# A spectral layer behind attention: two spectrum slots instead of three, four kw per mixing matmul, transposes behind each bank, stores on one queue

## The chip, the cores and the metric

The kernel runs on one core of a Trainium2 chip. The metric is the device time of one execution in microseconds. A core has five engines with queues of their own: TensorE (PE; its weight loads are listed as PEld), VectorE (DVE), ScalarE (ACT), GpSimd (POOL) and SyncE (SP). SP, ACT and POOL also issue DMAs: an issue stands in order in its engine's queue, and the profile shows it under SPq, ACTq or POOLq. A line number such as L198 is a line of the kernel before.

## The reference

The input x has shape (4, 64, 96, 96). Two layers follow each other, both on a group-normalised input and both added to it.

```python
# layer 0, N = 9216 places, 8 channels for q and k
energy = einsum('bcn,bcm->bnm', Q, K)
att = sigmoid(energy)
out = einsum('bcm,bnm->bcn', V, att) + x
out = out * sigmoid(mlp(mean(out)) + mlp(max(out)))
# layer 1
u_hat = rfft2(u, norm='ortho')
top = einsum('bchw,cohw->bohw', u_hat[:, :, :16, :16], R_pos)
bot = einsum('bchw,cohw->bohw', u_hat[:, :, H-16:, :16], R_neg)
# v_hat is zero but for top and bot
y = irfft2(v_hat, s=(H, W), norm='ortho')
```

R_pos and R_neg are complex, 64 by 64 channels for each of 16 x 16 frequencies. Layer 1 thus uses 32 frequencies kh along the height and 16 frequencies kw along the width. All numbers are float32.

## The kernel before, in words

The four images are worked on in two pairs; the 128 partitions hold 2 images x 64 channels. Layer 0's attention runs over 2 pairs x 18 blocks of 512 query places x 24 bursts of 6 key tiles, 864 bursts in all. In a burst PE computes six energy tiles for the next burst (L420), ACT takes their sigmoid (L424), and PE multiplies the sigmoids of this burst by the values (L431). Other work is hung on bursts by lists (`mid`, `end`) that `place(offset, every, steps)` fills by hand. Pair 0's layer 1 (`Hidden`) is hung on the bursts of pair 1. Pair 1's layer 1 has no attention left to hide in and follows it, from L583 on: "the tail". Within the tail, Tile's scheduler may reorder instructions that don't depend on each other. Each engine's queue is then fixed and worked off in order.

Layer 1 has these stages, in both forms.

- **Forward along w and h.** PE multiplies by constants of cosines and sines. In the tail, DVE transposes blocks of 32 x 32 in between (L629, L643), with three buffers xt (L628); PE accumulates the two images' spectra in `pu` (L648).
- **Spectrum.** The spectrum is scaled by the normalisation (`rs`, from `spread`) and written into `ut` in the form in which the mixing needs it as a stationary operand: 128 partitions are (real or imaginary part) x (64 input channels), columns are kh x kw x 3 slots x 2 images. The slots hold the three variants of real and imaginary parts from which the mixing makes minus the imaginary part, the real part and the imaginary part of the result. In the tail this takes transposes of `pu` into its own order and with the two halves of the partitions swapped (L680 to L682), two scalings on ACT (L684, L685) and one on DVE (L686) for each image; `sign` (L671) holds the factors. In `Hidden` it is `along_h` with L299 and L301. `constant_mode` (L181) corrects the constant mode.
- **Mixing** (`mix`, L183 to L224). For each group q of four kh and each half of the kw, PE multiplies 32 columns of `ut` by the weights of two kw side by side (L198): 128 columns of moving operand, 4 kh in the four groups of 32 output partitions, 4 pairs of kw, so 16 matmuls for each PSUM bank. A float32 matmul is two records in the profile. Twelve of the 32 rows of a group are of use (2 kw x 6); products of one kw's spectrum with the other's weights are made and not read. The bank is copied to `vm` (in the tail by DVE and ACT in turn, L111 and L113; in `Hidden` by DVE alone), and after the second half the rows of each kh are stored to a DRAM tile `vd` (L209), 48 KB each: four stores, in the tail on SP and ACT in turn. After four q, the rows are read back as `vt` (L223), with kh on the partitions and the right blocks picked: eight loads of 64 KB, on SP and ACT in the tail, on SP in `Hidden`. The tail has three buffers `vm`.
- **Back along h.** PE multiplies `vt` by the constants `gh` (L709, in `Hidden` L314). `vt` stands twice (e = 0 and 1, for the real and the imaginary part of the result), in two arrangements of real and imaginary rows; `gh` is one block of 96 columns. In the tail the result fills eight PSUM banks, and DVE then transposes four banks of one image at a time into `z` (L713). In `Hidden` it goes through DRAM (`zd`), and `gh` has the rows h in an order such that each of four reads takes a run of rows.
- **Back along w.** PE multiplies by `gw` (L723, in `Hidden` L335), DVE adds the result to x1 (L727, L337), and the output is stored. In the tail, three PSUM tiles of 384 columns are made for each of 8 groups g, DVE adds each by itself, and after every second g three stores of 384 KB go out on SP and ACT in turn.

The weights of the mixing, 512 KB for each kh, are loaded by POOL in the tail: seven kh into places of their own and nine into x0's place ahead of time, nine into the place of `vT` while the tail runs, and seven into places of the tail's working tiles as these come free (L596, L656).

Of the kernel before, what the change touches and what calls it, by code (L numbers as in the profile page):

```python
# [40 lines left out]
P = 128  # L41
# [13 lines left out]
U = KH * KW * 6  # L55
UPAD = 26
# [8 lines left out]
SECOND = {"w1": 2 * R, "w2": P, "ident": P, "fw": 2 * KW, "fh": 4 * KH, "gh": H, "gw": 4 * W}  # L65
# [6 lines left out]
NSLOT = 7  # L72
NLATE = 3 * NSQ * P + H
# [3 lines left out]
def tile_kernel(ctx: ExitStack, tc: tile.TileContext, x, cst, late, spec, out):  # L77
# [67 lines left out]
    class Layer1:  # L145


        def __init__(self, p, gate, bank, move, queues):
            self.p, self.gate, self.bank, self.move, self.queues = p, gate, bank, move, queues
            self.vd = dram.tile([KH, 12, 2, KW // 2 * C], F32, tag=f"vd{p}", name=f"vd_{p}")  # L150
            self.vt = None
# [24 lines left out]
        def constant_mode(self):  # L176

            for rows, slot, op in ((slice(0, C), 1, ALU.add), (slice(C, P), 2, ALU.add),
                                   (slice(C, P), 0, ALU.subtract)):
                at = self.ut[rows, 2 * slot:2 * slot + 2]  # L180
                nc.vector.tensor_tensor(at, at, self.rs[rows, 2, :], op)  # L181

        def mix(self, q, half):  # L183
# [7 lines left out]

            pv = self.bank(f"pv_{self.p}_{q}_{half}")
            K4 = KW // 4
            for k in range(K4):
                kw = half * K4 + k
                for g in range(4):
                    at = ((4 * q + g) * KW + 2 * kw) * 6
                    nc.tensor.matmul(  # L198
                        pv[bass.ts(g, 32), :].rearrange("q (n k o) -> q n k o", n=2, o=C)[
                            :, :, k, :],  # L200
                        self.ut[:, at:at + 32],
                        self.wts[4 * q + g].rearrange("q (n k o) -> q n k o", n=2, o=C)[
                            :, :, kw, :], start=True, stop=True)
            vm = self.vms[q].rearrange("q (n m) -> q n m", n=2)
            self.move(vm[:, :, bass.ts(half, K4 * C)], pv.rearrange("q (n m) -> q n m", n=2))
            if half == 0:
                return
            for g in range(4):
                self.queues[g % 2].dma_start(  # L209
                    self.vd[4 * q + g].rearrange("s n m -> s (n m)"),  # L210
                    self.vms[q][32 * g:32 * g + 12, :])
            if q % 4 == 3:
                if self.vt is None:
                    self.vt = self.places_of_vt()
                row, M = 12 * KW * C, KW // 2 * C
                for b in range(2):
                    for part in range(2):
                        to = 64 * b + 32 * part + 4 * q - 12
                        for e in range(2):
                            of = self.vd[4 * q - 12, 2 * (1 - part + e) + b, 0, :]  # L220
                            of = bass.AP(tensor=of.tensor, offset=of.offset,
                                         ap=[[row, 16], [6 * KW * C + M, 2], [1, M]])
                            self.queues[e + 1].dma_start(  # L223
                                self.vt[e][to:to + 16, :].rearrange("h (n m) -> h n m", n=2), of)  # L224

    class Hidden(Layer1):


        def __init__(self, p, gate, bank, move, queues, work):
            super().__init__(p, gate, bank, move, queues + queues[:1])  # L230
# [6 lines left out]
        def places_of_vt(self):  # L237
            vt = self.work.tile([P, 2, KW * C], F32, tag="ah", name=f"vt_{self.p}")
            return [vt[:, 0, :], vt[:, 1, :]]
# [22 lines left out]
        def along_w(self, m):  # L262
# [10 lines left out]
            for g in range(4):  # L273
                self.queues[0].dma_start(
# [3 lines left out]
            self.queues[1].dma_start(self.ah[rows, :],  # L278
                                     self.ad[rows].rearrange("h k c -> h (k c)"))

        def along_h(self, i):
# [3 lines left out]
            u = self.ut[:, :U].rearrange("q (h k s b) -> q h k s b", k=KW, s=3, b=2)  # L285
# [532 lines left out]
```

## Time and profile before

| what | value |
|---|---|
| time, median of 3 runs | 3213.67 us (3213.33 to 3218.87) |
| profiled execution, its own time | 3214.8 us |
| its span | 3213.0 us |
| PE busy (matmuls) | 3145.4 us, 98% |
| ACT busy | 2435.0 us, 76% |
| DVE busy | 405.3 us, 13% |
| L431, attention times values | 10368 records of 601 ns |
| L420, energies | 5184 records of 460 ns |
| L198, mixing of pair 0 | 512 records of 273 ns (median) |
| mean granted clock of TensorE | 0.992 |

The span is the time from the first to the last instruction of the execution that was profiled; the 1.8 us more in its own time lie around it. Busy shares are averages over the whole span. As the attention fills nearly all of it, they say little of the tail, which has to be read by itself: from the end of the attention (about 3105 us) to 3213.0. The mean duration of a matmul record includes its way through the array, and records overlap, so a rate is read from the starts of consecutive records and not from the durations.

### The profile page before, as it was taken

To read this page: it belongs to the slowest core of one execution; us is meant where nothing else is said; L and a number is where in the kernel's file an instruction comes from. 1 tells how busy PE (TensorE), PEld (TensorE's weight loads), DVE (VectorE), ACT (ScalarE), POOL (GpSimd) and SP (SyncE) were. 2 spreads that over 40 slices of the span, in tenths; PEclk is the share of its full clock that TensorE was granted. 3 is DMA by queue.
4 is the path that set the end of the run, shared out by engine and by line. 5 is a ranking of instruction groups with operands and counts; after the bars stand their busy time and mean duration, and the time that the engine had idled before them with its cause. 6 is when DMAs were issued, how large, how long until landed. Compare 5 with 4: busy or idle time off the path is not lost.

```text
span 3213.0 us, 40155 instructions
## 1 busy us (share of the span) xinstructions
PE 3145.4 (98%) x17960; PEld 1076.8 (34%) x17960; DVE 405.3 (13%) x856; ACT 2435.0 (76%) x1767; POOL 20.3 (1%) x41
## 2 busy tenths in 40 slices
PE   7999999999999999999999999999999999999985
PEld 3333333333333333334333333333333333333334
DVE  5200000000000000003231110000000110000034
ACT  3788888888888888886777777777777777888861
POOL 0000000000000000000000000000000001000000
PEclk9999999999999999999999999999999999999997
DMA  3000000000000000000120101211010013000034
GB/s 138 1 1 1 1 1 1 1 1 1 1 1 1 1 1 1 1 1 1 40 92 16 38 1 43 75 63 39 16 24 20 30 40 133 1 1 1 16 98 144
DMA packets 38973, 86.85 MB, mean 27 GB/s; under 512 B 10672, under 2 KB 16816, under 8 KB 38704
## 3 DMA queue, kind: packets, MB, share of 16 engines
q1 hardware_dynamic: 31696, 60.83, 6.4%
q0 software_dynamic: 4752, 17.42, 1.5%
q10 hardware_dynamic: 2352, 6.04, 0.6%
q8 instruction: 140, 2.29, 0.3%
q14 instruction: 33, 0.27, 0.0%
HBM read 63.82 MB, written 20.45 MB: 26 GB/s over the span
## 4 chain that ended last, share of the span: by engine, by line
PE 97%; DVE 1%; DMA 1%; issue 0%; ACTq 0%; ACT 0%; SPq 0%; DVEq 0%; POOL 0%
PE acc L431 73%; PE e L420 18%; PE pv L390 1%; PE pv L198 1%; PE py L335 1%; PE pq L401 1%; PE pk L381 0%; DMA x<-in_x_dram 0%; PE py L723 0%; PE pt L257 0%; DVE x L156 0%; PE pz L314 0%; DVE xt L629 0%; DMA vt<-vd 0%; DMA vd<-vm 0%
## 5 line engine op out<-in xcount | busy, mean ns | idle before, releaser
L424 ACT ACTIVATE at<-e 128x1536 f32<-128x1536 f32 x1728 | 2412.4, 1448 | 682.1 <-PE e L420 682.1
L431 PE MATMUL acc<-at,vT 128*64 128x512 f32 x10368 | 2417.6, 601 | 0.0
L431 PEld LDWEIGHTS acc<-at,vT 128*64 128x64 f32 x10368 | 667.9, 136 | 1294.7 <-issue 1279.5
L420 PE MATMUL e<-q,kT 32*128 32x512 f32 x5184 | 635.7, 460 | 2.0 <-ACT at L424 1.3
L420 PEld LDWEIGHTS e<-q,kT 32*128 32x128 f32 x5184 | 257.2, 182 | 638.8 <-issue 588.6
L361 DVE TENSOR_SCALAR full_q<-pq,cs 128x256 f32<-128x256 f32 x36 | 17.4, 484 | 1556.7 <-PE pq L401 1556.6
L575 DVE SCALAR_TENSOR_TENSOR x<-acc,x 128x512 f32<-128x512 f32 x36 | 24.9, 692 | 293.7 <-PE acc L431 293.7
L390 PE MATMUL pv<-cs,x 128*128 128x128 f32 x288 | 42.9, 292 | 0.2
L337 DVE TENSOR_TENSOR x<-py,x 128x384 f32<-128x384 f32 x24 | 13.4, 558 | 226.1 <-PE py L335 226.1
L411 DVE CAST q<-q 32x256 fp32r<-32x256 f32 x144 | 41.0, 285 | 3.8
L390 PEld LDWEIGHTS pv<-cs,x 128*128 128x128 f32 x288 | 35.7, 195 | 14.1 <-DVE full_k L361 12.9
L510 DVE COPY ws<-pv 128x512 f32<-128x512 f32 x16 | 11.1, 691 | 216.4 <-PE pv L198 216.4
L369 DVE SCALAR_TENSOR_TENSOR q<-high_q,cs,full_q 64x256 fp32r<-64x256 f32 x72 | 34.6, 481 | 2.4
L510 DVE COPY xT<-pt 96x512 f32<-96x512 f32 x24 | 16.4, 685 | 114.4 <-PE pt L257 114.4
L361 DVE TENSOR_SCALAR full_k<-pk,cs 128x256 f32<-128x256 f32 x36 | 17.4, 484 | 102.0 <-PE pk L381 102.0
L392 DVE TENSOR_TENSOR vT<-pv,cs 128x512 f32<-128x512 f32 x36 | 24.9, 691 | 8.8 <-PE pv L390 8.8
L577 DVE TENSOR_REDUCE maxs<-x 128x1 f32<-128x512 f32 x36 | 24.7, 685 | 1.1
L381 PE MATMUL pk<-x,cs 128*64 128x256 f32 x144 | 23.0, 390 | 1.5 <-DVE x L143 1.5
L637 PE MATMUL pa<-xt,lc 128*128 128x256 f32 x72 | 20.0, 432 | 3.4 <-DVE xt L629 3.4
L438 DVE BATCH_NORM_STATS2 stats<-x 128x6 f32<-128x512 f32 x36 | 22.2, 679 | 7.9 <-DMA x<-in_x_dram 7.9
L401 PE MATMUL pq<-x,cs 128*64 128x256 f32 x144 | 22.1, 386 | 0.0
L335 PE MATMUL py<-cs,ws 128*128 128x384 f32 x48 | 21.9, 538 | 0.0
(99 smaller groups left out, 450.2 us busy)
## 6 DMA issues: line engine op xcount, KB each, us to landing
ws<-in_spec_dram SPq DMA_DIRECT2D x32, 512.0 KB
x<-in_x_dram SPq DMA_DIRECT2D x15, 512.0 KB
out_dram<-x SPq DMA_DIRECT2D x18, 384.0 KB
w<-in_spec_dram POOLq DMA_DIRECT2D x10, 512.0 KB, 4.9
old<-in_x_dram SPq DMA_DIRECT2D x12, 384.0 KB
x1d<-x SPq DMA_DIRECT2D x12, 384.0 KB
x<-x1d SPq DMA_DIRECT2D x12, 384.0 KB
w_early<-in_spec_dram POOLq DMA_DIRECT2D x9, 512.0 KB, 9.1
```

What stands on the lines that cost most here:

```text
L198: nc.tensor.matmul(pv[bass.ts(g, 32), :].rearrange("q (n k o) -> q n k o", n=2, o=C)[:, :, k, :], self.ut[:, at:at + 32], self.wts[4 * q + ...
L335: nc.tensor.matmul(py[:, :4 * W], self.z[:, i, :], named("gw"), start=True, stop=True)
L361: nc.vector.tensor_scalar(u, src, bias, None, ALU.add)
L369: mark[0] = nc.vector.scalar_tensor_tensor(dst, h.bitcast(F32), is_low, u, ALU.mult, ALU.add)
L390: nc.tensor.matmul(pp[:, bass.ts(i, P)], xs[p][:, bass.ts(4 * s + i, P)], named("wv"), start=True, stop=True)
L392: nc.vector.tensor_tensor(vT[:, 4 * s:4 * s + 4, :], pp.rearrange("p (i m) -> p i m", m=P), named("bv").unsqueeze(1).to_broadcast([P, 4, P ...
L401: nc.tensor.matmul(pq[rows, :half], named("wq")[:, rows], xs[p][:, n * NB + e * half:n * NB + (e + 1) * half], start=True, stop=True)
L411: nc.vector.tensor_copy(q[to:to + 32, cols], q[of:of + 32, cols])
L420: nc.tensor.matmul(eb[i // PART][:, i % PART, :], kT[r:r + 32, t // 4, :], q[r:r + 32, :], start=True, stop=True)
L424: nc.scalar.activation(at[:, bass.ts(h, PART), :], eb[h], AF.Sigmoid)
L431: nc.tensor.matmul(acc[half, :], vT[:, j, half], at[:, i, :], start=(j == 0), stop=(j == NCH - 1))
L510: l1 = Hidden(0, gate, bank_a, lambda dst, src: nc.vector.tensor_copy(dst, src), (nc.sync, nc.sync), work)
```

## The change

The spectrum `ut` has two slots (the real part's and the imaginary part's product) instead of three. The minus sign moves into `gh`, which gets two blocks, one for each e, and `vt` stands once. In the mixing, SIDE = 4 kw lie side by side: a matmul has the same 32 columns of stationary operand, of which 16 are now of use, and 256 columns of moving operand, and a bank takes 2 x 4 matmuls instead of 4 x 4. A store of `vd` has 16 rows (64 KB) instead of 12, and all of them are on SP; four loads of `vt`, in pieces of 1 KB, take the place of eight in pieces of 2 KB. In the tail the loads after q = 3 are on POOL, those after q = 7 on SP and ACT. There are four `vm` and four xt.

Back along h in the tail goes by groups of 16 output channels: for each group, two e and two images, matmuls of 256 columns that read `vt` with a step of 64 elements, each image's group into a bank of its own; behind each bank stands a transpose of 512 elements. Back along w, one addition takes the three PSUM banks of a g, and the three stores follow it. One kh less is loaded ahead of time (NSLOT 6) and one more late. In `Hidden`, the two scalings of `along_h` are split by n instead of by slot, and the reads of `zd` take every fourth row, as `gh` has its rows in plain order.

```diff
-U = KH * KW * 6
-UPAD = 26
+SIDE = 4
+U = KH * KW * 4
+UPAD = 4 * SIDE
...
-            for k in range(K4):
-                kw = half * K4 + k
+            for k in range(2):
+                kw = half * 2 + k
                 for g in range(4):
-                    at = ((4 * q + g) * KW + 2 * kw) * 6
+                    at = ((4 * q + g) * KW + SIDE * kw) * 4
...
             for g in range(4):
-                self.queues[g % 2].dma_start(
-                    self.vd[4 * q + g].rearrange("s n m -> s (n m)"),
-                    self.vms[q][32 * g:32 * g + 12, :])
+                nc.sync.dma_start(self.vd[4 * q + g], self.vms[q][32 * g:32 * g + 4 * SIDE, :])
...
                 for b in range(2):
-                    for part in range(2):
-                        to = 64 * b + 32 * part + 4 * q - 12
-                        for e in range(2):
-                            of = self.vd[4 * q - 12, 2 * (1 - part + e) + b, 0, :]
...
+                    for slot in range(2):
+                        to = 64 * b + 32 * slot + 4 * q - 12
+                        of = self.vd[4 * q - 12, 2 * slot + b, :]
...
+                        self.load_queue(q, slot).dma_start(
+                            self.vt[to:to + 16, :].rearrange("h (n m) -> h n m", n=SIDE), of)
...
-                    evacuate, (nc.sync, nc.scalar, nc.sync))
+                    evacuate, lambda q, slot: nc.gpsimd if q == 3 else (nc.sync, nc.scalar)[slot])
...
-            xt = place_of(f"t{s % 3}", f"xt_{s}")[:, :STRIP]
+            xt = place_of(f"t{s % 4}", f"xt_{s}")[:, :STRIP]
...
-            nc.vector.transpose(own, pu[b])
-            nc.vector.transpose(swapped[:C, :], pu[b][C:, :])
-            nc.vector.transpose(swapped[C:, :], pu[b][:C, :])
...
+            nc.vector.transpose(tb, pu[b])
+            tb = tb.rearrange("q (n k h) -> q n k h", n=SIDE, h=KH)
+            nc.scalar.activation(u[:, :, :, :, 0, b], tb, AF.Copy, scale=l1.rs[:, 0, b:b + 1])
+            nc.vector.tensor_scalar(u[lo, :, :, :, 1, b], tb[hi], l1.rs[hi, 1, b:b + 1], None,
+                                    ALU.mult)
+            nc.vector.tensor_scalar(u[hi, :, :, :, 1, b], tb[lo], l1.rs[lo, 0, b:b + 1], None,
                                     ALU.mult)
...
-        l1.vms = [tail.tile([P, KW * C], F32, tag="vm", bufs=3, name=f"vm_{q}")
+        l1.vms = [tail.tile([P, KW * C], F32, tag="vm", bufs=4, name=f"vm_{q}")
...
+        for i in range(4):
+            for e in range(2):
+                for b in range(2):
+                    rows = bass.ts(b, 2 * KH)
+                    nc.tensor.matmul(
+                        pz[b][i][:H, :].rearrange("q (o e k) -> q e o k", e=2, k=KW)[:, e],
+                        named("gh")[rows, bass.ts(e, H)],
+                        l1.vt[rows, :].rearrange("q (k o) -> q o k", o=C)[:, bass.ts(i, NO), :],
+                        start=True, stop=True)
+        z = tail.tile([P, SQ, P], F32, tag="z", name="z_1")
         for i in range(4):
             for b in range(2):
-                rows = bass.ts(b, 2 * KH)
-                nc.tensor.matmul(pz[b][:H, bass.ts(i, NB)], gh[rows],
-                                 l1.vt[i // 2][rows, bass.ts(i % 2, NB)], start=True, stop=True)
-        z = tail.tile([P, SQ, P], F32, tag="z", name="z_1")
-        for b in range(2):
-            nc.vector.transpose(z[:H, :, bass.ts(b, C)].rearrange("q h o -> q o h"),
-                                pz[b][:H, :].rearrange("q (k o) -> q o k", o=C))
+                nc.vector.transpose(
+                    z[:H, :, b * C + i * NO:b * C + (i + 1) * NO].rearrange("q h o -> q o h"),
+                    pz[b][i][:H, :])
...
-            for j in range(NSQ):
-                part = x1[:, bass.ts(j * (SQ // HG) + g, HG * W)]
-                nc.vector.tensor_tensor(part, py[j][:, :HG * W], part, ALU.add)
-                if g % 2:
+            nc.vector.tensor_tensor(rows_of[:, g], py[:, :, :HG * W], rows_of[:, g], ALU.add)
+            if g % 2:
+                for j in range(NSQ):
```

## The prediction

> **What bounds the kernel now.** I read the shares by engine and the slices of the page first, then the chain that ended last, then the busy time by stretch, and last the timeline of the stretches that the change touches.
>
> ```profile
> PE 3145.4 (98%) x17960; PEld 1076.8 (34%) x17960; DVE 405.3 (13%) x856; ACT 2435.0 (76%) x1767; POOL 20.3 (1%) x41
> ...
> PE 97%; DVE 1%; DMA 1%; issue 0%; ACTq 0%; ACT 0%; SPq 0%; DVEq 0%; POOL 0%
> ```
>
> TensorE (PE) carries 97% of the chain, nearly all of it attention (L431, L420). Pair 0's spectral layer is hidden there by DVE and the queues, but its matmuls lie on PE's own path. Pair 1's spectral layer stands bare behind the attention, from 3105 to 3213 us. So there are two questions: what the change does to PE inside the attention, and what it does to the bare 108 us. For the first, the timeline of PE around one hidden mixing step:
>
> ```profile
> 1950.29 0.73 PE L420 MATMUL e<-q,kT 32*128 32x512 f32 x6
> 1950.95 2.79 PE L431 MATMUL acc<-at,vT 128*64 128x512 f32 x12
> 1953.68 1.08 PE L198 MATMUL pv<-ws 128*32 128x128 f32 x32
> 1954.69 0.73 PE L420 MATMUL e<-q,kT 32*128 32x512 f32 x6
> ```
>
> A burst with a half step of mixing lasts 1954.69-1950.29 = 4.40 us; without one, 3.39 (1950.29-1946.90). So each of the 16 half steps costs 1.01 us of end time. For the second, the bare stretch cut where its releasers stand (columns: stretch, length, busy time of PE, PEld, DVE, ACT, POOL, then clock, DMA share, GB/s):
>
> ```profile
> 3142.30:3149.84 7.54, 0.32 (x8) 0.26 (x9) 6.90 (x19) 4.45 (x4) 1.10 (x2) 0.82 0.33 109
> 3149.84:3179.19 29.35, 16.54 (x512) 16.03 (x513) 5.53 (x8) 4.68 (x8) 0.53 (x1) 0.79 0.59 118
> 3179.19:3192.82 13.63, 7.35 (x16) 3.64 (x16) 7.03 (x2) 0.00 (x0) 0.00 (x0) 0.75 0.01 2
> 3192.82:3213.00 20.18, 14.15 (x192) 13.91 (x192) 11.89 (x24) 0.00 (x0) 0.00 (x0) 0.50 0.61 235
> ```
>
> These are spectrum, mixing with its round trip through DRAM, back along h, back along w. In the first DVE is the bound, 6.90 of 7.54. In the second PE works 16.5 of 29.4 and is idle for the last 12. In the third PE and DVE work strictly one after the other: 7.35+7.03 is more than 13.63. In the fourth PE is busy at half clock. Why the second is so long, the timeline of ACT shows:
>
> ```profile
> 3162.55 0.58 ACT L113 COPY vm<-pv 128x512 f32<-128x512 f32 x1 [0.65 <-PE pv L198]
> 3162.61 0.30 ACTq L209 DMA_DIRECT2D vd<-vm  x1
> 3163.20 2.75 ACTq L223 DMA_DIRECT2D vt<-vd  x4
> 3167.48 1.90 ACTq L209 DMA_DIRECT2D vd<-vm  x3
> 3169.42 0.58 ACT L113 COPY vm<-pv 128x512 f32<-128x512 f32 x1 [6.29 <-DMA vt<-vd]
> 3170.20 0.58 ACT L113 COPY vm<-pv 128x512 f32<-128x512 f32 x1 [0.20 <-DMA vd<-vm]
> ```
>
> ACT empties a PSUM bank only after the stores and first loads queued ahead on it, and the third vm buffer is not free before its stores land. PE's last product (3166.6) thus waits until 3170.2 to be copied. The chain behind it:
>
> ```profile
> 3171.58 2.88 DMA vd<-vm
> ...
> 3175.51 3.67 DMA vt<-vd
> ...
> 3179.19 6.52 PE pz L709 x13
> ...
> 3185.74 7.04 DVE z L713 x2
> ```
>
> **The change, part by part**, against the profiled execution (span 3213.0, time 3214.8, so 1.8 around it).
>
> *Hidden part: 0.* A half step has 16 matmul records of 256 columns instead of 32 of 128, four side by side either way. The tail's mixing at full clock starts one 128-column record every 27 ns, 108 ns for four, 0.85 ns a column. The 512-column acc matmuls take 2.73 us for 12, two side by side: 0.455 us, 0.89 ns a column. Narrow ones cost no more per column, so the 1.01 us stays. Bounds: half of 16.2 us if the count decided (-8), +1 if a longer chain delays a burst. I keep 0 because equal columns are the nearest row. Evictions stay 16; the back matmuls (L314) keep shape and number; along_h's DVE pair (1.125+0.64 us) becomes two of 256 elements; vt loads halve. ACT's and PE's attention work covers these DVE and SP edits (DVE is 13% busy); uncovered, they would be under 2 us in all.
>
> *Spectrum: 7.54 to 5.05, saves 2.5.* Four 64-partition transposes (0.71 each), four sign copies (0.69 together), two L686 of 0.66, one constant addition and two ACT scalings (1.17 each) go. DVE keeps two transposes (0.72 each), the four rs operations (0.42 together), four scalings on 64 partitions at L686's 0.65, and two additions (0.35): 1.44+0.42+2.60+0.35 = 4.8, with handoffs 5.05. ACT's two scalings of 1.15 fit beside. If the scalings cost like L299 (1.125), +1.9; if ACT's chain decides, -0.6. Mixing starts at 3147.35. POOL's last two weight loads are issued some 2 us earlier, 14 us before their use.
>
> *Mixing and round trip: 29.35 to 24.05, saves 5.3.* Columns are unchanged, so PE needs its 16.5 us less the stalls late in it and part of its 4 us at half clock: 15.5, to 3162.85. ACT has no store ahead of its copies and vm has four buffers, so the last copy ends 0.75 later. SP has all 32 stores. In the hidden part it issues four from 1966.80 to 1967.95, 0.38 apart, 1.5 us per q against PE's 1.75 (full clock), so it keeps up. Behind SP's stores stand only its two last vt loads, for which PE waits; the first half's four loads move to POOL, behind the weights, where nobody waits. Last store issued at 3164.75; landing 2.9 as before; semaphores and issue 0.45; two loads per queue instead of four. Before, 4.5 us passed from the first such issue (3174.68) to PE's start; the bytes are half, the pieces as many but 1 KB long. Taken 3.3: PE starts at 3171.4. Bounds: PE wholly at full clock 13.9 (-1.6), loads 2.7 to 4.5 (-0.6, +1.2), stores 0.55 apart as L209's longest on SP (+3.3, since 8x4x0.55 = 17.6 then outlasts PE). Stores carry 16 rows instead of 12, in rows of 4 KB as before.
>
> *Back along h: 13.63 to 8.8, saves 4.8.* PE streams as many columns: 16x512 records, two side by side, 4096 x 1.67 ns = 6.8 at half clock; the clock rose 5.4 us in, so about 6.4. In four groups of 1.7, two banks each. Eight DVE transposes of 512 elements: between 0.72 (L680, plain rows) and 0.94 (L643's 1877 ns for 1024, strided on both sides); the write stays strided, the PSUM read turns plain: 0.83. First group 1.9, then 8x0.83 = 6.65, handoffs 0.25: 8.8. The moving operand is now read with a step of 64 elements, which no matmul here does. Nearest is ACT's scaling with strided writes, 1.16 us for 512, 2.27 ns each against 0.58 us plain. By it PE needs 9.3 and the stage 11 (saves 2.6); by twice the half-clock rate, 13.7 and 15.3 (loses 1.7). I take 1.67, because a half-clock column already takes longer than a strided element on DVE (0.66 us/512 = 1.29 ns).
>
> Against this change speaks the Trainium skill's page "SBUF — State Buffer" (section "Door 1: The DMA port swizzle"): only accesses within one 16-byte line run at full bandwidth, each crossing pays. It gives no size; by doubling, the sum below would shrink by the 6.5 us just bounded.
>
> *Back along w: 20.18 to 19.9, saves 0.3.* One addition over 1152 elements replaces three of 384: from 550 ns for 384 and 692 for 512 follow 1.40 us against 1.49. But the six first stores wait for the whole addition (up to 0.8 us), and the last three start together at the end: +0.7 with PE at half clock. PE ran this whole stage at clock 0.50 although busy, having idled 6.3 us before. Now it idles 2.3 us and may begin at full clock. Then DVE (8x1.33) and the stores decide: 4.7 MB at the 390 GB/s reached at the end is 12.1 us, and the stage shrinks by 2.1. Nothing shows whether this sparse work holds a clock it can't raise; I take a value between.
>
> "TensorE: Matmul & The Clock Gate" (Part 1) says sustained activity of some 3.4 us raises the clock. This stage, 14 us busy at 0.50, speaks against it; by the rule the stage would run at full clock, and the sum would be 1.8 larger.
>
> The first bare stretch to 3142.3 keeps its operations; a fourth xt buffer finds DVE already the chain: 0, within 1 either way.
>
> **Sum:** 0+2.5+5.3+4.8+0.3 = 12.9: span 3200.1, profiled time 3201.9. The median of the runs shown (3213.67) lies 1.1 under the profiled time: 3200.8.
>
> **Rivals.** (1) PE stays at full clock in mixing and back along w: 1.6+1.8 more, 3197.4. For: shorter idle times; against: the last stage never left half clock. 0.18. (2) The strided moving read doubles back along h: 3207.3. For: ACT's doubled scaling; against: DVE's strided write cost only 0.66 against 0.54. 0.14. (3) One queue bounds the mixing at 0.55 us per store: 3204.1. For: L209 on SP took 0.54 to 0.56 in the mixing; against: two queues issued together then, 0.38 alone. 0.13. (4) The change doesn't do what it says: copies are still held up by another wait and the round trip gains nothing: 3206.1. 0.05. (5) Slower: that strided read at four times the half-clock price, 6.7 ns a column, adds 20.5 us: 3221.3. It decides from 1.67+12.9/4096 us, 4.8 ns a column, for no gain, and from 6.4 for a loss of 0.2%. Against: no strided row here costs over 2.3 ns. 0.05. Forecast 0.45.
>
> 0.2% is 6.4 us, about what a measurement tells from no change: below 3207.3 is faster. Half of (2) lies within 0.2%, with some of (4): faster 0.87, same 0.08, slower 0.05. The range takes in (1), (3), (4) and (2) to its middle, with the spectrum's and loads' bounds partly combined: 3195.5 to 3207.5.
>
> **What would show it.** Bursts with mixing still 4.40 us. First bare mixing matmul near 5 us after the last pu. No ACT copy waiting on a vt load. PE's idle time between mixing and pz 8.5 instead of 12.6. DVE transposes (0.8 each) beginning 2 us into pz. The prediction falls if pz records take over 1 us per 256 columns, if SP's stores lag PE by several us, or if bursts with mixing change.

## The result, and the profile after

| | before | after |
|---|---|---|
| time, median of 4 runs each | 3214.59 us (3213.33 to 3218.87) | 3205.20 us (3203.89 to 3206.90) |
| profiled execution, its own time | 3214.8 us | 3205.57 us |
| its span | 3213.0 us | 3203.8 us |

One run of the kernel before, made beside the changed one, has joined the three of the table above. The changed kernel is faster by 9.4 us: the ratio is 0.9969, with a 95% interval of 0.9951 to 0.9986. The time lies inside the range given; of the 12.9 us worked out, the profiled spans show 9.2. Lines are now those of the kernel after: L426 and L415 are the attention (before L431, L420), L198 the mixing, L209 the stores, L220 the loads of `vt`, L700 and L708 back along h, L720 and L722 back along w, L114 ACT's copies. In a kernel of an experiment these numbers shift by the lines that its edit adds.

The chain of the page, by engine, as in the line shown of before:

```profile
PE 97%; DVE 1%; DMA 1%; SPq 0%; issue 0%; ACT 0%; POOL 0%; ACTq 0%
```

SPq has moved from the seventh place to the fourth, ahead of ACT and ACTq: a first hint that the bare part now waits for SP's queue. The busy time by stretch, cut at the same events (first row: from the end of the attention to the end of `pu`; then spectrum, mixing with its round trip, back along h, back along w; columns as before):

```profile
3105.59:3142.14 36.55, 26.64 (x106) 18.36 (x108) 29.80 (x45) 12.04 (x25) 8.60 (x16) 0.89 0.62 217
3142.14:3146.89 4.75, 0.49 (x9) 0.43 (x10) 4.37 (x12) 2.08 (x2) 0.66 (x2) 0.50 0.51 183
3146.89:3173.45 26.56, 15.97 (x257) 9.35 (x257) 5.53 (x8) 4.68 (x8) 2.51 (x5) 0.82 0.56 120
3173.45:3182.65 9.20, 7.91 (x33) 5.96 (x33) 7.12 (x8) 0.00 (x0) 0.00 (x0) 0.74 0.00 0
3182.65:3203.80 21.15, 12.77 (x192) 12.35 (x192) 10.77 (x8) 0.00 (x0) 0.00 (x0) 0.56 0.58 225
```

Cut exactly at the records, that gives:

| stretch | before | after | gained | predicted |
|---|---|---|---|---|
| start to end of attention | 3105.01 | 3105.54 | -0.5 | 0 |
| to the end of `pu` | 37.28 | 36.56 | 0.7 | 0 |
| spectrum | 7.55 | 4.79 | 2.8 | 2.5 |
| mixing and round trip | 29.35 | 26.56 | 2.8 | 5.3 |
| back along h | 13.63 | 9.20 | 4.4 | 4.8 |
| back along w | 20.18 | 21.14 | -1.0 | 0.3 |
| sum | 3213.0 | 3203.8 | 9.2 | 12.9 |

Two stretches hold the difference of 3.7 us: mixing (2.5 short) and back along w (1.3 short). The hidden part did what was forecast. The timeline of PE around a hidden mixing step of the kernel after:

```profile
1951.13 0.73 PE L415 MATMUL e<-q,kT 32*128 32x512 f32 x6
1951.79 2.80 PE L426 MATMUL acc<-at,vT 128*64 128x512 f32 x12
1954.52 1.07 PE L198 MATMUL pv<-ws 128*32 128x256 f32 x16
1955.52 0.73 PE L415 MATMUL e<-q,kT 32*128 32x512 f32 x6
```

The burst lasts 1955.52-1951.13 = 4.39 us, as before (4.40), with 16 records of 256 columns in the place of 32 of 128. Here PE pays for columns, not for matmuls.

Where the mixing's gain went, the chain that ended last shows. Columns: start, length, what. The parts left out are SP's other stores, and further down the handoffs between the rows:

```profile
3153.23 0.30 SPq L209
...
3154.04 1.35 SPq L209
...
3158.22 0.42 SPq L209
...
3158.68 0.42 SPq L209
...
3161.01 1.45 SPq L209
...
3167.82 2.14 DMA vd<-vm
...
3170.21 2.99 DMA vt<-vd
...
3173.45 2.01 PE pz L700 x6
```

From 3153.23 to 3167.82 the chain is nothing but L209 on SP: fourteen and a half microseconds in which SP issues one store after another, each 0.46 from the next (3158.68-3158.22), and twice 1.35 and 1.45 us for one. PE's last mixing product was done at 3162.86 and its copy at 3163.55, both where the prediction had them (3162.85, 3163.6). The last store was issued 4.3 us after that copy. In the kernel before ACT's copies waited for their queue; now they don't. Three of them still wait for a `vm` buffer whose stores have to land first (3.5 us in all), but the last copy ends where it was expected, and the queue of the stores is the wait.

### The profile page after: what moved, and what is told of

It reads as the page before. It is cut to its first block, busy times and chain, and to the rows that moved or that the text cites. A ratio compares the mean times of both kernels' runs of the same rounds, so it can differ in the third digit from the quotient of the medians.

```text
span 3203.8 us, 39104 instructions
## 1 busy us (share of the span) xinstructions
PE 3144.6 (98%) x17464; PEld 1065.2 (33%) x17464; DVE 399.8 (12%) x838; ACT 2432.9 (76%) x1765; POOL 22.4 (1%) x45
## 4 chain that ended last, share of the span: by engine, by line
PE 97%; DVE 1%; DMA 1%; SPq 0%; issue 0%; ACT 0%; POOL 0%; ACTq 0%
PE acc L426 74%; PE e L415 18%; PE pv L385 1%; PE pv L198 1%; PE py L330 1%; PE pq L396 1%; PE pk L376 1%; DMA x<-in_x_dram 0%; PE pt L253 0%; SPq L209 0%; PE py L720 0%; PE pz L309 0%; PE pa L631 0%; PE pu L290 0%; DVE z L708 0%; PE pu L642 0%
## 5 line engine op out<-in xcount | busy, mean ns | idle before, releaser
L426 PE MATMUL acc<-at,vT 128*64 128x512 f32 x10368 | 2418.0, 601 | 0.0
L426 PEld LDWEIGHTS acc<-at,vT 128*64 128x64 f32 x10368 | 667.8, 136 | 1294.5 <-issue 1279.1
L415 PE MATMUL e<-q,kT 32*128 32x512 f32 x5184 | 636.0, 461 | 1.9 <-ACT at L419 1.3
L415 PEld LDWEIGHTS e<-q,kT 32*128 32x128 f32 x5184 | 257.5, 182 | 642.8 <-issue 591.2
L385 PEld LDWEIGHTS pv<-cs,x 128*128 128x128 f32 x288 | 35.7, 195 | 14.2 <-DVE full_k L356 12.9
```

The lines of the kernel that those rows point to most:

```text
L385: nc.tensor.matmul(pp[:, bass.ts(i, P)], xs[p][:, bass.ts(4 * s + i, P)], named("wv"), start=True, stop=True)
L415: nc.tensor.matmul(eb[i // PART][:, i % PART, :], kT[r:r + 32, t // 4, :], q[r:r + 32, :], start=True, stop=True)
L426: nc.tensor.matmul(acc[half, :], vT[:, j, half], at[:, i, :], start=(j == 0), stop=(j == NCH - 1))
```

## The experiments

All times are medians; "before" is the kernel before on the same chip. An interval of a ratio spans some 6 to 11 us between its ends, as the kernel before scatters over 5 us; so the readings below rest on the stretches, and times are compared within one chip. Where the same code ran again, the stretches repeat so: mixing 26.56, 26.66, 26.78, 27.51 (the kernel after, e13, e7, e3); spectrum 4.78 to 4.82; back along h 9.19 to 9.25; the first stretch 35.9 to 36.9; the end of the attention 3104.2 to 3106.6 us. Part of the mixing's scatter is the clock: each mixing begins at half clock, which lasts another 2.6 us (e5) to 5.5 us (e1), and PE's own part, from its first product to its last, takes 15.5 us in the one and 16.7 in the other (16.0 in the kernel after).

**The changed kernel again (e13).** It was run beside three others, to have it on their chip.

> The changed kernel itself, unedited, beside e10 to e12 on one chip. If the long issue of the last output store on ACT (1.94 us) recurs, its last stage is 21 to 21.2 us, else near 20.2; the stretch from the first mixing matmul to the first pz matmul is 26.3 to 26.9 us. By the other edits its time should lie 4 to 5 us above e10_last_q.

It took 3205.82 us (3204.20 to 3206.95); before 3215.11; ratio 0.9970 (0.9958 to 0.9981). The stretches are 26.66, 9.25 and 20.17 us. So the mixing is no accident of one execution, while one microsecond of the last stretch is: here it is 20.2 instead of 21.1. Here too two issues of SP are long (1.55 and 1.42 us).

**Stores on two queues (e1).** The change's single queue is undone for pair 1, all else stays.

```diff
-                nc.sync.dma_start(self.vd[4 * q + g], self.vms[q][32 * g:32 * g + 4 * SIDE, :])
+                (nc.sync, nc.scalar if self.p else nc.sync)[g % 2].dma_start(
+                    self.vd[4 * q + g], self.vms[q][32 * g:32 * g + 4 * SIDE, :])
```

> The changed kernel with one edit: in the tail, the mixing's stores go on SP and ACT in turn again, 16 each. Theory (SP's issue sets the end of the mixing stage: 32 stores 0.46 us apart, the last one issued 4.3 us after the last copy out of PSUM, 3167.82 against 3163.55): with two queues the last store is issued about 1.6 us after the last copy, the stretch from the first mixing matmul to the first pz matmul shrinks from 26.56 to about 24 us, and the time falls by 2 to 3 us against the changed kernel. ACT has two stores (0.95 us) and a copy (0.58) per q against PE's 1.75, so its copies stay in time. Rival (the stores' way through the DMA engines is the bound, whichever queue issues them; the engines' share is 0.45 to 0.87 there): the stretch stays at 26 to 27 us and the time doesn't move.

3202.18 us; before 3215.27; ratio 0.9959 (0.9944 to 0.9974). The mixing took 24.93, 1.6 less than with one queue. The last store was issued 0.86 after the last copy instead of 4.3. But the last copy ended 18.2 us after the stretch began instead of 16.7. Of these 1.5 us PE's longer half clock makes 0.8. The rest lies between PE's last product and the end of its copy, 1.4 us instead of 0.7: ACT issued stores until 0.1 us before that copy, and the profile puts the copy's wait down to the landing of a store. Which of the two held it was not separated. So the theory's direction held, and the full 2.5 did not come.

**One store of 128 rows per q (e2).** SP issues 8 stores instead of 32, in the hidden part too; half of the rows stored are never read. `vd` is laid out to fit.

```diff
...
-            for g in range(4):
-                nc.sync.dma_start(self.vd[4 * q + g], self.vms[q][32 * g:32 * g + 4 * SIDE, :])
+            nc.sync.dma_start(self.vd[q], self.vms[q])
...
```

> The changed kernel with one edit: for each q one store of all 128 rows of vm (512 KB, half of it rows that nobody reads) instead of four stores of 16 rows; vd is laid out to fit; in the hidden part too. SP issues 8 stores instead of 32. Theory (number of issues on SP): the last store goes out within 0.2 us of the last copy, the stretch shrinks from 26.56 to 23.5 to 24.5 us, the time by 2 to 3 us. Rival (the DMA engines): twice the bytes keep the stretch at 26.5 us or make it longer.

3202.91 us; before 3215.27; ratio 0.9960 (0.9945 to 0.9975). SP is free: the last store was issued 0.02 after the last copy. The mixing still took 24.94, because that one store landed 4.1 us after its issue, against 2.1, and PE itself took 0.6 us longer, with more of it at half clock. Twice the bytes kept the DMA engines no busier, as the DMA queues of the window from 3150 to 3170 us show (packets, MB, share of 16 engines). The kernel after:

```profile
q1 hardware_dynamic: 1024, 2.10, 56.6%
```

This kernel:

```profile
q1 hardware_dynamic: 1232, 4.27, 54.9%
```

A packet of 4 KB took 328 ns (median) in a store of 16 rows and 160 ns in one of 128.

**Three queues' worth on two (e6).** SP takes three of four stores and ACT the last one (two of the last q); the three additions of the kernel before are back too.

```diff
-                nc.sync.dma_start(self.vd[4 * q + g], self.vms[q][32 * g:32 * g + 4 * SIDE, :])
+                queue = nc.scalar if self.p and (g == 3 or (q == 7 and g == 2)) else nc.sync
+                queue.dma_start(self.vd[4 * q + g], self.vms[q][32 * g:32 * g + 4 * SIDE, :])
...
```

> The changed kernel with two edits: three additions per g back along w, and of the mixing's four stores per q one on ACT and three on SP (two and two for the last q). Theory (SP's 0.46 us per store is the bound of the mixing's end, and the joint addition that of the output's): SP needs 1.4 us per q against PE's 1.75, the last store is issued under 1 us after the last copy, the stretch from the first mixing matmul to the first pz matmul takes 23.0 to 23.7 us (26.56 with one queue, 24.93 with stores in turn), the last stage 20 to 20.2; the time is 4 to 4.5 us under the changed kernel, near 3201. Rival (the landings of these small stores are the bound, whichever queue): the stretch stays at 24.9 as with both earlier edits, time near 3202.5.

3204.53 us; before 3216.18; ratio 0.9964 (0.9951 to 0.9978). The theory fell: the mixing took 27.51, no better than with one queue, though SP had 23 stores instead of 32. What SP waited for between 3155 and 3175 us (total, times, longest):

```profile
SPq L210 <- DMA vd<-vm: 4.2, 4, 1.7
```

A store waited for the landing of an earlier store. At 3168.04 it was that of ACT's store of 3164.64, whose semaphore the waiting store uses again; SP was idle for 1.7 us, though its data were ready. The kernel after has no such row of SP. So a second limit lies close behind the issue time: stores in flight. The chain that ended last passes through four landings of stores (1.90, 2.99, 3.94 and 2.07 us), which is why cutting only the issues on SP does not help here. Some of e1's miss may lie there as well (1.7 us on two such waits). The same queues took 27.16 in e9 and 28.19 in e8, below.

**One wide store, and four small ones at the end (e10).** What e2 and e6 taught, put together: few stores (no wait for a landing), but the last q in pieces of 16 rows on two queues, which land sooner; three additions as before the change. `vd` is laid out to fit.

```diff
...
-            for g in range(4):
-                nc.sync.dma_start(self.vd[4 * q + g], self.vms[q][32 * g:32 * g + 4 * SIDE, :])
+            if q < 7 or not self.p:
+                nc.sync.dma_start(self.vd[q], self.vms[q])
+            else:
+                for g in range(4):
+                    rows = slice(32 * g, 32 * g + 4 * SIDE)
+                    (nc.sync, nc.scalar)[g % 2].dma_start(self.vd[q, rows, :], self.vms[q][rows, :])
...
```

> The changed kernel with three additions per g back along w, one store of 128 rows per q for the first seven q (as in e2_one_store), and for the last q four stores of 16 rows, two on SP and two on ACT. Theory (SP's issues up to the last q, then the landing of the last store, set the mixing's end): the last store is issued 0.5 us after the last copy, lands 2.5 us later as with two queues (4.2 with one store of 512 KB), and the stretch from the first mixing matmul to the first pz matmul takes 22.8 to 23.6 us (26.56 in the changed kernel, 24.94 with one store). With the last stage at 19 to 20 the time is 4 to 5 us under the changed kernel. Rival (the earlier 512 KB stores are still in flight and delay the last four): 24.5 us or more, as with one store.

3201.12 us (3199.95 to 3201.68); before 3215.11; ratio 0.9955 (0.9942 to 0.9967). This is the fastest kernel of the study, 14.0 us under the kernel before and 4.7 under the changed one of the same chip, whose runs begin at 3204.20. The chain at the end of its mixing:

```profile
3162.79 0.36 ACTq L213
...
3163.18 3.32 DMA vd<-vm
...
3166.60 3.00 DMA vt<-vd
```

SP no longer appears. The mixing took 24.27, between the theory's and the rival's number: the small stores queue behind the wide ones' transfers and land after 3.3 us, where 2.5 was counted on. In e11, below, the same stores landed after 2.95 us and the half clock was 1.4 us shorter: 23.20.

**The kernel before with q = 3's loads on POOL (e5).** This is the smallest edit that frees ACT's copies, made on the kernel before.

```diff
-                            self.queues[e + 1].dma_start(
+                            (nc.gpsimd if self.p and q == 3 else self.queues[e + 1]).dma_start(
```

> The kernel before with one edit: in the tail, the eight vt loads after q = 3 are on POOL instead of SP and ACT. Theory (ACT's copies stood behind the loads that wait for the stores of q = 3): the copy that waited 6.29 us for them goes at once, the stretch from the first mixing matmul to the first pz matmul shrinks from 29.35 to about 26.5 us and the time by 2.5 to 3 us. Rival (the three vm buffers, free only when the stores have landed, hold the copies as long): the stretch stays above 28.5 us.

3211.33 us; before 3215.27; ratio 0.9989 (0.9979 to 0.9998). The mixing with its round trip:

```profile
3151.30:3176.88 25.58, 15.46 (x513) 15.22 (x513) 5.54 (x8) 4.69 (x8) 4.57 (x9) 0.83 0.60 134
```

It fell from 29.35 to 25.57, more than expected. ACT's last copy moved from 3171.05 to 3167.38 and its last store from 3171.58 to 3168.06; some 0.7 us of the gain is the clock's, whose half lasted 2.6 us here against 4.1. One line thus shortens the mixing further than the whole change does (26.56).

**The same, with all stores on SP (e12).** Added to e5:

```diff
-                self.queues[g % 2].dma_start(
+                self.queues[0].dma_start(
```

> The kernel of e5_before_pool_loads (the kernel before with the loads after q = 3 on POOL) with one more edit: all stores of the mixing on SP, as in the change. Theory (one queue's issue is the cost): stores of 12 rows take 0.36 to 0.40 us on SP, four of them 1.6 against PE's 1.75 per q, so only the last q's stores come later, and the two refills of SP's instructions cost 1 us each: the stretch from the first mixing matmul to the first pz matmul rises from 25.57 to 26.2 to 27.5 us. Rival (one queue costs nothing; what was long in the changed kernel is the longer store of 16 rows): 25.4 to 25.9.

3214.67 us; before 3215.11; ratio 0.9998 (0.9989 to 1.0007): what e5 had gained is gone. The mixing takes 27.88, 2.3 more than e5's, somewhat more than expected:

```profile
3150.67:3178.55 27.88, 15.97 (x512) 15.73 (x513) 5.53 (x8) 4.68 (x8) 4.54 (x9) 0.81 0.57 124
```

Of the 2.3, PE's longer half clock makes 0.5. The chain shows L209 on SP from 3158.51 on, and then two landings:

```profile
3162.78 1.55 SPq L209
...
3166.89 4.85 DMA vd<-vm
...
3171.75 2.09 DMA vd<-vm
```

The last copy ended at 3167.96 and the last store was issued 3.8 us later. Three issues took over a microsecond each (1.03, 1.55, 1.47), and the last store then waited 0.5 us for the landing of an earlier one, as in e6. So one queue for the stores costs some 2 us also where a store has 12 rows, without the rest of the change.

**Three additions (e3).** Only the joint addition is undone; `py` is again three tiles of their own.

```diff
...
-            nc.vector.tensor_tensor(rows_of[:, g], py[:, :, :HG * W], rows_of[:, g], ALU.add)
+            for j in range(NSQ):
+                part = x1[:, bass.ts(j * (SQ // HG) + g, HG * W)]
+                nc.vector.tensor_tensor(part, py[j][:, :HG * W], part, ALU.add)
...
```

> The changed kernel with one edit: back along w uses three PSUM tiles and three additions of 384 elements for each g again, each store right behind its addition. Theory (the joint addition delays the first stores and bunches the last three; the stage took 21.15 us against 20.18 before although it began at full clock): the stage falls to about 20.2 us, the time by about 0.9. Rival (the longer stage comes from the last ACT store's issue of 1.94 us, which has nothing to do with the addition): stage within 0.4 of 21.15 if such an issue recurs there, near 19.7 if it falls elsewhere.

3203.71 us; before 3215.27; ratio 0.9963 (0.9949 to 0.9977). Back along w took 19.98. That run alone can't settle it, because the clock fell at 3181.1, just ahead of this stretch; in the kernel after it fell 2.4 us into it. Over all runs the pattern is clear. With a joint addition and a start at full clock: 20.16, 20.22, 20.17, and 21.14 and 21.06 where ACT's last output issue took 1.9 us. With three additions and a start at full clock: 18.93, 19.11, 19.40, 19.12. With three additions and half clock throughout: 19.98, 21.19, and 20.18 before (20.18 and 20.17 in e5 and e12). So the joint addition costs about a microsecond, and a start at full clock is worth about one (19.1 against 20.2; the 21.19 is taken up under e11).

**Three xt (e7).** The fourth xt buffer of the first stretch is taken back.

```diff
-            xt = place_of(f"t{s % 4}", f"xt_{s}")[:, :STRIP]
+            xt = place_of(f"t{s % 3}", f"xt_{s}")[:, :STRIP]
```

> The changed kernel with one edit: xt has three buffers again instead of four. The stretch from the end of attention to the last pu matmul took 37.28 us in the kernel before and 36.56 in the changed one, 35.9 in three variants of it. Theory A (the fourth buffer does it): the stretch goes back to 37.3 or more, the time rises by 0.7 to 1.5 us. Theory B (the phase of the clock's change does it; nothing there waits for a buffer): the stretch stays at 35.9 to 36.6.

3205.16 us; before 3216.18; ratio 0.9968 (0.9955 to 0.9980). The first stretch took 37.03, 0.1 above what four buffers gave (35.9 to 36.9). The buffer is worth nothing that this can tell.

**PE kept busy, with the strided read (e9) and with a plain one (e8).** Both have e6's queues and three additions. Nine matmuls of 512 columns, whose product nobody reads, are put behind the mixing, to raise or hold the clock for back along h. In e8 moreover PE reads `vt` in runs of 16 elements and DVE takes over the reordering. With that PE's results, too, go to PSUM in one run of 256 elements, where the kernel after and e9 write them in runs of 16 with gaps:

```diff
+        spare = l1.bank("spare")
+        for i in range(9):
+            nc.tensor.matmul(spare, ident, x1[:, bass.ts(i, NB)], start=True, stop=True)
...
-                        pz[b][i][:H, :].rearrange("q (o e k) -> q e o k", e=2, k=KW)[:, e],
+                        pz[b][i][:H, :].rearrange("q (e k o) -> q e k o", e=2, k=KW)[:, e],
...
-                        l1.vt[rows, :].rearrange("q (k o) -> q o k", o=C)[:, bass.ts(i, NO), :],
+                        l1.vt[rows, :].rearrange("q (k o) -> q k o", o=C)[:, :, bass.ts(i, NO)],
...
-                    pz[b][i][:H, :])
+                    pz[b][i][:H, :].rearrange("q (c o) -> q o c", o=NO))
```

> The kernel of e6_both with the nine dense matmuls of e8_warm_plain alone; pz reads vt with its step of 64 as in the changed kernel. Theory (the strided read holds PE at 1.69 ns a column whatever the clock): pz records stand 0.217 us apart although the clock is full, and the stage stays at 9.0 to 9.3 us. Rival (the half clock alone made them 0.217 apart; the 0.217 after the clock's rise in the changed kernel came from somewhere else): 0.11 apart, first transpose after 1.1 us, stage near 8.1.

> The kernel of e6_both with two more edits: nine dense matmuls of 512 columns, whose product nobody reads, between the last mixing matmul and the first pz matmul, so that PE doesn't idle 10 us there; and pz reads vt in runs of 16 elements instead of with a step of 64, with DVE's transposes reading PSUM with a step of 16 instead. Theory (the strided read costs 1.69 ns a column at either clock; plain reads cost 0.85 at full clock): the clock is full when pz begins, pz records stand 0.11 us apart instead of 0.217, the first transpose starts 1.1 us after pz instead of 2.03; the transposes (0.87 to 0.94 each) then are the bound and the stage falls from 9.2 to 8.1 to 8.7 us. Rival (the strided PSUM read slows the transposes to over 1 us each): 9.2 or more.

e9: 3203.58 us, ratio 0.9963 (0.9949 to 0.9976); e8: 3203.39 us, ratio 0.9964 (0.9952 to 0.9977); before 3216.18. Back along h took 9.18 and 8.98. The clock was not held: the added matmuls ended 3.7 and 3.8 us before `pz`, and it fell at 3173.1 in e9, as `pz` began, and in e8 at 3174.2, 0.7 us later. But it rose again within the stage, and so the price of the read at full clock can be seen. The busy time of the records of `pz`, cut at the clock's rise (stretch, length, busy time and records of PE, PEld, DVE, then the clock, DMA share, GB/s), first at full clock in the kernel after:

```profile
3178.23:3181.30 3.07, 3.07 (x14) 1.59 (x10) 3.07 (x5) 1.00 0.00 0
```

The same of e9, at full clock:

```profile
3176.48:3180.80 4.32, 4.32 (x20) 2.81 (x17) 4.32 (x6) 1.00 0.00 0
```

And of e8, up to the rise and from it on:

```profile
3173.52:3177.60 4.08, 4.08 (x19) 3.12 (x21) 2.44 (x3) 0.58 0.00 0
3177.60:3179.40 1.80, 1.80 (x15) 1.18 (x11) 1.80 (x3) 1.00 0.00 0
```

At full clock the strided form (the kernel after, e9) yields a record per 0.22 us (4.32/20), as at half clock; the plain one (e8) needs 0.22 while the clock is mostly at half (4.08/19) and, at full clock, 0.22 per two (0.11 each, from the starts of the records 3177.66 to 3178.52; the row's mean holds the pause in front of the last ones). So the strided form does cost double, but only at full clock; at half clock it is hidden. That it is the read and not the write in runs of 16 is not shown: no run changes one without the other.

**The same in a shorter mixing (e11).** e10's stores and additions, six such matmuls, and the plain read.

> The kernel of e10_last_q with the plain read of vt and six dense matmuls of 512 columns, whose product nobody reads, between mixing and pz. The nine of e8_warm_plain ended 3.5 us before pz and the clock fell as pz began; here PE should be idle under 2 us. Theory (at full clock and read plainly, pz records stand 0.11 us apart, so that DVE alone bounds the stage): first transpose 1.1 us after pz begins, eight transposes 0.86 to 0.9 us apart, stage 8.0 to 8.4 us instead of 9.2, the time 0.8 to 1.2 under e10_last_q. Rival (the clock still falls before or in pz): 8.9 to 9.2, no gain.

3201.80 us; before 3215.11; ratio 0.9958 (0.9945 to 0.9970), no faster than e10. Back along h took 8.90; the records of `pz` in its first two parts, cut at the clock's changes:

```profile
3169.58:3170.50 0.92, 0.92 (x6) 0.74 (x8) 0.00 (x0) 0.99 0.00 0
3170.50:3173.90 3.40, 3.40 (x18) 2.82 (x17) 2.76 (x3) 0.50 0.00 0
```

The stage did begin at full clock, which then fell 0.9 us in. The rival held: the first transpose began 1.15 us in, as the theory had it, but the second only 1.47 us behind it, as PE went on at half clock; the other six stood 0.85 to 0.90 apart. What was won there (0.3 us against e10) and in the mixing (1.1) was lost elsewhere: the first stretch took 0.8 longer, and back along w 21.2 instead of 19.1. There the clock had fallen at 3177.3, ahead of the stage, and the last addition ended 15.5 us in instead of 14.4. The other 0.9 lies behind that addition (5.7 instead of 4.8 us), with no issue on ACT or SP over 0.34 us: the last output moved for a microsecond at 12 to 37 GB/s. Why was not tried.

## Why the prediction was right, and where its size was off

**Right in sign and mechanism.** *Hidden part, 0:* confirmed by the bursts (4.39 and 4.40 us). *Spectrum, 2.5:* 2.8; DVE is the bound as worked out, 4.37 us busy of 4.75, where 4.8 had been counted. *Back along h, 4.8:* 4.4. The kernel before did not work there "strictly one after the other", as the prediction reads it: 7.35+7.03 in 13.63 is an overlap of 0.75. PE's strided form took 1.69 ns a column against the 1.67 that was chosen, and rival 2 (a doubled price) did not decide the stage. That was luck of the clock in part: the form does cost double at full clock (e8 against e9), and half clock hides it for half of the stage. DVE's transposes, put at 0.83 apart, came 0.87 apart, which explains some 0.3 of the 0.4 missing.

The Trainium skill's page "SBUF — State Buffer" (section "Door 1: The DMA port swizzle"), weighed in the prediction, says that a step across 16-byte lines costs. The runs agree with it as far as they go: double at full clock and nothing at half clock, for the strided read and the write in runs of 16 together.

**The step that failed: mixing, 5.3, of which 2.8 came.** It is the sentence "1.5 us per q against PE's 1.75 (full clock), so it keeps up". The end of PE's work and of the last copy held to 0.1 us (PE began 0.5 earlier and took 0.5 longer). SP then lagged by 4.3 us instead of 1.2, for three reasons, which add up. From SP's first store at 3151.20 to its last at 3167.82 are 16.6 us: 31 steps of 0.46 make 14.3, the two long issues add 0.9 and 1.0, and a pause of 0.34 ahead of the last two stores the rest. The price of 0.38 was read from stores of 12 rows; those of 16 rows take 0.41 to 0.42 to issue, with 0.04 between, and four take 1.85 us per q, more than PE's 1.75. At 0.46 without a long issue the last store would have stood at 3165.5, 0.7 later than predicted; the long issues made most of the rest. In e12 stores of 12 rows lagged by 3.8 us all the same, with three long issues. Behind the last store the round trip was 1.0 us shorter than worked out (2.1 instead of 2.9 to land, 0.25 instead of 0.45 for semaphores and issue, loads as predicted). The prediction had named this sign itself: it "falls [...] if SP's stores lag PE by several us", and in this part it did; PE's idle time ahead of `pz` was 10.6 us, not 8.5.

This is rival 3's mechanism, given a chance of 0.13: one queue bounds the mixing. Its price of 0.55 a store, 3.3 us more, was off in its parts (0.46 and two long issues); of it 2.5 came. The total lies inside the range because the range had taken this rival in, not because the sum was right. That it is the queue, and not the rest of the change, was shown from both sides: taking stores off it saves 1.6 to 2.4 (e1, e2, e10), and putting them on it costs 2.3 in the kernel before (e12 against e5), 0.5 of it the clock's. What makes the long issues long stays open. That stores also wait for earlier landings (e6) was not in the prediction at all.

**Back along w, 0.3; it lost 1.0.** Both effects that the prediction set against each other are there. The stage began at full clock and ended its last addition 14.8 us in, not 15.5: 0.7 won. (The joint addition, put at 1.40 us and further down at 1.33, took 1.36.) But from the last addition to the end of the span passed 6.4 us instead of 4.7. The stage of the kernel after, cut at the clock's fall and at the end of the last addition:

```profile
3182.65:3185.03 2.38, 2.03 (x48) 1.87 (x48) 1.18 (x1) 0.00 (x0) 0.00 (x0) 1.00 0.00 0
3185.03:3197.41 12.38, 10.73 (x144) 10.48 (x144) 9.59 (x8) 0.00 (x0) 0.00 (x0) 0.50 0.71 277
3197.41:3203.80 6.39, 0.00 (x0) 0.00 (x0) 0.00 (x0) 0.00 (x0) 0.00 (x0) 0.50 0.54 207
```

The last two of these parts in e10:

```profile
3181.40:3193.43 12.03, 10.91 (x142) 10.67 (x142) 10.63 (x22) 0.00 (x0) 0.00 (x0) 0.50 0.76 297
3193.43:3198.20 4.77, 0.00 (x0) 0.00 (x0) 0.00 (x0) 0.00 (x0) 0.00 (x0) 0.50 0.61 243
```

With three additions two of the last three stores start before the last addition ends, and 4.8 us remain (4.7 before); with one addition all three start behind it, and 5.4 remain (e13), or 6.4 where ACT's last issue took 1.94. The prediction had put this end at 0.7, and it is; the long issue adds 1.0 in some executions. The gain it hoped for was cut off by the clock, which held for 2.4 us and then fell, though PE was at work. The question left open ("whether this sparse work holds a clock it can't raise") is answered in part: in no run did full clock outlast the first 2.4 us of this stage, but the 3.41 us up to the fall also held most of PE's pause of 1.3 us ahead of it, so that unbroken work of this kind was not tried. What it doesn't do is raise the clock: from 3187 to 3195 us the profile lists PE as busy without a gap, at 0.50. The Trainium skill's page "TensorE: Matmul & The Clock Gate" (Part 1), by whose rule sustained activity raises the clock, does not hold for this stage in any run, if a PE listed as busy is taken for activity.

**The first stretch, 0 within 1:** it gained 0.7 and the attention's end gave back 0.5. Both lie within the spread of kernels that share this code, and the fourth xt shows no effect (e7).

## What to carry to other kernels

Before work is gathered on one queue, price each issue with the shape that it will have, add what the queue issues between, and compare the sum with the producer's pace; a queue that only just keeps up is lost at the first long issue. A stall that is removed is worth only what the next wait leaves: one moved group of loads in the kernel before (e5) freed 3.8 us of mixing, and the gathered stores gave a part back. Few wide stores for what has time to land, and small ones on several queues for the last, was the best of the ways tried.

## What the runs showed of the hardware

- **The issue time of a store.** Back to back, most of the second and later of four stores took 0.36 to issue with 12 rows (e12) and 0.42 with 16. It doesn't simply grow with the rows: e2's stores of 128 rows, one at a time, took 0.32 to 0.33.
- **A 4 KB packet took longer in stores of few rows:** 328 ns with 16 rows, 333 with 12 (e12), 160 with 128. A 512 KB store of 128 rows takes the DMA engines no longer than four of 64 KB, but lands after 4.1 us instead of 2.1.
- **Long DMA issues beside instruction packets.** The issues of 1.35 and 1.45 us on SP began at 3154.04 and 3161.01; packets of 16 KB on the queue "instruction" at 3154.11 and 3161.17. ACT's 1.94 began at 3197.85, with such a packet at 3198.03. e12's and e13's overlap with such packets in the same way, but not every packet goes with a long issue: beside e12's of 3155.09 SP's issues took 0.33 to 0.36. With 8 stores instead of 32 (e2) no issue in the mixing was long. That the packets cause them was not tried by itself.
- **Matmuls with a strided moving read** (steps of 64 float32) that also write PSUM in runs of 16 take 1.69 ns a column at either clock, plain ones 1.67 at half clock and 0.84 at full. The two were not separated.
- **The clock.** Its changes lie multiples of 3.41 us apart in every trace: in the kernel after at 3167.97, 3178.20 and 3185.03 (10.23 and 6.83 apart, three and two times 3.41), in e11 at 3170.49, 3173.90 and 3177.32 (3.41 and 3.42). So an edit ahead can move the clock of the stages behind, as in e11, where back along w began 1.2 us after a fall and its additions took 15.5 us instead of e10's 14.4. That the place alone decides is not shown: PE had also been idle longer ahead of it (2.8 us).
